# Graph attention on one core: addresses read a run ahead, one-hots of two batches, sums of sixteen tiles

## The chip, the cores and the metric

The kernel runs on one core of a Trainium2 chip. The metric is the device time of one execution in microseconds. The names of the engines are those of the profile: PE (TensorE, with PEld for its weight loads), DVE (VectorE), ACT (ScalarE), POOL (GpSimd, here the issuer of the gathers), SP (issuer of most DMAs).

## The reference

A graph has 6250 nodes with 128 features and 206250 directed edges, sorted by destination, of which each has 128 features too. Every edge takes a key and a value from its source node, a query from its destination node and a factor from its own features; there are eight heads of 16.

```python
score = jnp.einsum('ehd,ehd,ehd->eh', Kh[src], Qh[dst], Eh) * inv_sqrt_d
score = jnp.exp(jnp.clip(score, -5.0, 5.0))
msg = Vh[src] * score[:, :, None]
wV = jax.ops.segment_sum(msg, dst, num_segments=N)
Z = jax.ops.segment_sum(score, dst, num_segments=N)
h_out = wV / (Z[:, :, None] + 1e-06)
x = _layernorm(x + h_out)
```

## The kernel before

**Tiles and batches.** The edges are cut into 1612 tiles of 128 (one edge a partition), and these into 406 batches: 401 of four tiles, then small ones. The loop at L591 goes over the batches and works on several at once: for batch b it issues PE's products (`stage_a`, L463), for batch b-1 DVE's (`stage_b`, L478) and ACT's exps (`weigh`, L493), for batch b-2 the messages (`messages`, L523) and their sums (`stage_c`, L530).

**What a batch needs.** `gather` (L410) has POOL fetch the key and value rows of each tile's source nodes, one indirect DMA a tile, into one of 12 buffers `kvrows`. For batches from 12 on the rows come from the table kv, which the kernel builds at the start (`table`, L270: PE's `kvacc`, copies `kvst` by ACT and DVE, stores by SP); the first 12 batches gather rows of x and project them. A gather of batch b also waits for the PE product `qps` of batch b - lag(b), where lag (L360) falls from 12 to 3. For 163 tiles, the last ones of chosen batches, no gather is issued: ACT (88 columns, L392) and DVE (40 columns, L389, two at a time) copy columns of x from SBUF into a tile `xcol`, by addresses that each engine loads into its registers (L382, TENSOR_LOAD, eight addresses a run), and PE projects them (L401); ACT copies the result (L408).

**The chain of one batch.** PE makes `eps` = edge features times WE (L471, one PSUM buffer) and `qps` = queries spread over the edges (L474), whose left side is the one-hot `onehotT` (`stage_0t`, L454: DVE compares bf16 offsets `relb` with a node number). DVE then multiplies kq = kvrows × qps (L481) and kqe = kq × eps (L484), sums over a head (L487) and clips (L490). ACT takes the exp twice (L497, L498), DVE multiplies msg (L525), PE adds msg into `agg` (L547) with the one-hot `onehot` (`stage_0`, L444: DVE compares 64 node numbers with `rel`) on the left. Between these instructions `fill` (L583) puts single steps of other work on DVE: parts of the query table (`q_rows`, L301) and of finished blocks' layernorm (L741).

**Windows and sums.** Destinations are sorted, so a tile's nodes lie in a window of 64 from `window_start`. Four tiles share a window start; two groups of four (a pair, eight tiles) share one accumulator column, the second group 16 nodes on, with its 64 one-hot columns in the upper half of the 128; two such columns make an `agg` of 272 elements, which ACT copies to `sum` (L553). When all windows that touch two blocks of 128 nodes are there, `finish` (L513) has PE shift and add them into `finps` (L510), ACT copy that to `fin` (L520), and the layernorm steps are queued for the next round, the first of them rz (L749).

**What sets the order.** Up to batch 12 the framework orders the instructions; from then on (L592) each engine runs them in the order of the program. An instruction that waits holds up all behind it on its engine; SP's loads and stores are one such list, POOL's gathers another. Edge features (`ea`) are loaded in chunks of eight tiles into a ring of five buffers (L346).

**The window of destinations.** `from_window` (L183) prepares the bf16 offsets: it loads destinations (`dB_sb`), takes a bounded start (L191), subtracts (L194), stores the result to HBM (relD, read back as `relb`) and counts. Its first half runs while the tables are built, its second from batch 30 on, a step a batch.

Of the kernel before, what the change touches and what calls it, by code (L numbers as in the profile page):

```python
# [9 lines left out]
F32 = mybir.dt.float32  # L10
I32 = mybir.dt.int32
BF16 = mybir.dt.bfloat16
# [11 lines left out]
HW = 64  # L24
HALF = 16
DRIFT = 24
# [6 lines left out]
GLEAD = 2  # L33
OHB = (3, 5)
TAIL = 8
# [20 lines left out]
RING = 4096  # L56
SUMS = 8
XT_AT = RING + P
# [20 lines left out]

def pair_of(t):  # L80

    return (t // (2 * G), t // G % 2) if t < LAST else (NT, 1)


def pair_start(k):

    return (2 * k * G * N + NT // 2) // NT - DRIFT


def window_start(t):  # L90
    k, half = pair_of(t)
    return QL * P + HW if k == NT else pair_start(k) + HALF * half

# [7 lines left out]
def edge_attention(ctx: ExitStack, tc: tile.TileContext, x, xT, srcT, srcC, dstT, dstB, dst0, bnd, lo, eaT,  # L101
# [37 lines left out]
    with ExitStack() as fast:  # L139
# [7 lines left out]
        nc.gpsimd.iota(io2, pattern=[[1, P]], base=0, channel_multiplier=0)  # L147
        nc.vector.tensor_scalar(shift[:HW], io_i[:HW], 0, None, op0=ALU.is_equal)
        nc.vector.tensor_scalar(shift[HW:], io_i[HW:], HALF - HW, None, op0=ALU.is_equal)
        nc.vector.tensor_scalar(ident, io_i[:, P:2 * P], 0, None, op0=ALU.is_equal)  # L150
        for h in range(2):
            for tl in halves[h]:
                nc.vector.memset(tl[:, :, HW - HW * h:P - HW * h], 0.0)
        nc.vector.tensor_copy(iota_f, io2)
        dB_sb = [ip.tile([P, WT * P], I32, name="dB_sb", bufs=1)]
        nc.scalar.dma_start(dB_sb[0][:min(P, NJ)], dstB[:min(P, NJ)])
        bnd_c = ip.tile([P, (NJ + P - 1) // P], I32, name="bnd_c")
# [25 lines left out]
        def from_window(i):  # L183

            a, k = i * P, min(P, NJ - i * P)
            if i == len(dB_sb):
                dB_sb.append(ip.tile([P, WT * P], I32, name="dB_sb", bufs=1))
                nc.sync.dma_start(dB_sb[i][:k], dstB[a:a + k])
            d = dB_sb[i]
            w = ip.tile([P, 1], F32, name="wq0", bufs=2)  # L190
            nc.vector.tensor_tensor(w[:k], d[:k, :1], bnd_c[:k, i:i + 1], op=ALU.min)  # L191
# [172 lines left out]
        col_tiles, xT_bytes = {}, spread.bitcast(U8)  # L364
        used = [0, 0]

        copied, projected = {}, []

        def columns(eng, b, share=1.0):
# [5 lines left out]
            due = int((b - COL0 + COLL - 1 + share) * runs * COLP[1] / COLP[0] + 1e-6)  # L375
            while copied.get(engine, 0) < min(due, len(col_batches) * runs):
                k, j = divmod(copied.get(engine, 0), runs)
                copied[engine] = copied.get(engine, 0) + 1
                if k not in col_tiles:
                    col_tiles[k] = wp.tile([P, P], F32, name="xcol", bufs=4)  # L380
                to, j = col_tiles[k].bitcast(U8), first + j * size
                at = nc.values_load_multi_w_load_instructions(  # L382
                    col_at[k % col_half:k % col_half + 1, k // col_half, j:j + size], engines=(engine,),
                    min_val=XT_AT, max_val=XT_AT + 8 * (N - 1) + 4,
                    skip_runtime_bounds_check_because="edges name nodes")[1]
# [44 lines left out]
        def project(g, n):  # L430
# [6 lines left out]
            for i in range(0, n, 2):  # L437
# [4 lines left out]
                nc.scalar.copy(g[:, i:i + k, :], pk[:, :k, :])  # L442

        def stage_0(b):  # L444
            t0, n = batches[b][0], len(batches[b])
            half = pair_of(t0)[1]
            oh = halves[half][used[half] % OHB[half]]
            used[half] += 1
            nc.vector.tensor_tensor(oh[:, :n, HW * half:HW * half + HW],  # L449
                                    iota_p[:, None, :].to_broadcast([P, n, HW]),  # L450
                                    rel[:, t0:t0 + n, None].to_broadcast([P, n, HW]), op=ALU.is_equal)
            st8[b] = oh, None

        def stage_0t(b):  # L454
            t0, n = batches[b][0], len(batches[b])
            oh = st8[b][0]
            ohT = wp.tile([QROWS, B * P], BF16, name="onehotT", bufs=AHEAD + 2)
            e0 = t0 % RC * P
            nc.vector.tensor_scalar(ohT[:, :n * P], rels[t0 // RC][:, e0:e0 + n * P], node[:QROWS], None,  # L459
                                    op0=ALU.is_equal)  # L460
            st8[b] = oh, ohT

# [38 lines left out]
        def windows(q):  # L501

            return [(k, pair_start(k) - q * P) for k in range(min(NT, LAST + 2 * G - 1) // (2 * G))
                    if -HW - HALF < pair_start(k) - q * P < P]

        def add_windows(ps, q, first, stop):

            parts = windows(q)
            for i, (k, s) in enumerate(parts):
                nc.tensor.matmul(ps, shift[:, P - s:2 * P - s], sums[k // 2][:, k % 2],  # L510
                                 start=first and i == 0, stop=stop and i == len(parts) - 1)

        def finish(j):  # L513
# [5 lines left out]
            fin = sp.tile([P, 2, MW], F32, name="fin", bufs=2)  # L519
            nc.scalar.copy(fin, ps)  # L520
            pending.append(layernorm(nc, sp, fin, xbs.pop(q), out, q, 2, stores))

# [7 lines left out]
        def stage_c(b):  # L530
            n, g, oh, m = st8.pop(b)
            for i in range(n):
                t = batches[b][i]
                k, half = pair_of(t)
                q = t * N // NT // P
# [3 lines left out]
                final = k == NT  # L539
                u = k if final else k // 2  # L540
                first = u not in aggs
                if first:
                    aggs[u] = psA.tile([P, 2, MW], F32, name="agg")
                    if final:
                        add_windows(aggs[u][:, 0], QL, True, False)
                tail = k == NT if t == NT - 1 else pair_of(t + 1)[0] != k
                nc.tensor.matmul(aggs[u][:, 0 if final else k % 2], oh[:, i, :], m[:, i, :],  # L547
                                 start=not final and t % (2 * G) == 0, stop=tail)
                if tail and final:
                    norms.insert(0, layernorm(nc, sp, aggs.pop(u)[:, :1], xbs.pop(QL), out, QL, 1, stores))  # L550
                elif tail and (k % 2 == 1 or t == LAST - 1):
                    sums[u] = sp.tile([P, 2, MW], F32, name="sum", bufs=SUMS)
                    nc.scalar.copy(sums[u][:, :k % 2 + 1], aggs.pop(u)[:, :k % 2 + 1])  # L553
                    while len(finished) < QL // 2 and all(v // 2 <= u for v, _ in windows(2 * len(finished) + 1)):
                        ready.append(len(finished))
                        finished.append(u)

# [33 lines left out]
        for b in range(nbat + 3):  # L591
# [225 lines left out]
```

## Time and profile before

| what | us |
|---|---|
| median of 3 runs (1856.61 to 1858.39) | 1858.12 |
| the profiled execution | 1862.53 |
| its span | 1860.7 |
| busy in it: PE | 1330.8 |
| busy in it: DVE | 1680.8 |
| busy in it: ACT | 1632.9 |
| busy in it: POOL | 1385.7 |

The profile shows one execution. Its rows by group give line, engine, operation, output and inputs, count, then busy time and mean ns of one, then the engine's idle time before them and what ended it. Timeline rows give start, duration, engine, line, operation, and in brackets the idle time before with its releaser. Rows of stretches give the stretch, its length, an engine's busy time and instructions in it, the granted clock, the DMA share and GB/s. The moved bytes are 378.43 MB, 203 GB/s on average, and the granted clock is 0.922 on average.

### The profile page before, as it was taken

To read this page: it belongs to the slowest core of one execution; us is meant where nothing else is said; L and a number is where in the kernel's file an instruction comes from. 1 tells how busy PE (TensorE), PEld (TensorE's weight loads), DVE (VectorE), ACT (ScalarE), POOL (GpSimd) and SP (SyncE) were. 2 spreads that over 40 slices of the span, in tenths; PEclk is the share of its full clock that TensorE was granted. 3 is DMA by queue.
4 is the path that set the end of the run, shared out by engine and by line. 5 is a ranking of instruction groups with operands and counts; after the bars stand their busy time and mean duration, and the time that the engine had idled before them with its cause. 6 is when DMAs were issued, how large, how long until landed. Compare 5 with 4: busy or idle time off the path is not lost.

```text
span 1860.7 us, 48856 instructions
## 1 busy us (share of the span) xinstructions
PE 1330.8 (72%) x9376; PEld 1158.3 (62%) x9376; DVE 1680.8 (90%) x6913; ACT 1632.9 (88%) x15519; POOL 1385.7 (74%) x1456
## 2 busy tenths in 40 slices
PE   6887577677776777776776776766777767666776
PEld 4776466566665666665665665656666656656665
DVE  5589799999999999999999999989998999998987
ACT  2339689899999999999999999999999999998992
POOL 6777677777777777777777777777777777777774
PEclk7998799899999999999999899998898999998998
DMA  9776657667776576677677667667766676667662
GB/s 299 213 230 196 180 173 214 199 203 205 209 215 204 178 238 202 187 219 224 192 210 227 190 198 222 198 185 217 215 207 181 204 222 192 194 197 226 204 195 70
DMA packets 171231, 378.43 MB, mean 203 GB/s; under 512 B 58622, under 2 KB 84556, under 8 KB 170918
## 3 DMA queue, kind: packets, MB, share of 16 engines
q0 software_dynamic: 68768, 186.80, 34.6%
q1 hardware_dynamic: 101010, 187.38, 33.1%
q14 instruction: 237, 1.94, 0.3%
q8 instruction: 76, 1.25, 0.3%
q10 hardware_dynamic: 1140, 1.06, 0.2%
HBM read 360.30 MB, written 14.81 MB: 202 GB/s over the span
## 4 chain that ended last, share of the span: by engine, by line
DVE 43%; PE 11%; DMA 11%; issue 6%; DVEq 5%; POOL 4%; ACT 2%; ACTq 0%; POOLq 0%
DMA kvrows<-kv,src 11%; DVE kqe L484 8%; DVE kq L481 8%; DVE xcol L389 7%; DVE sc L487 5%; DVE msg L525 5%; DVEq L382 5%; PE eps L471 4%; DVE onehot L449 4%; POOL kvrows L419 4%; DVE onehotT L459 3%; PE finps L510 3%; PE agg L547 2%; DVE sc L490 1%; ACT xcol L392 1%
## 5 line engine op out<-in xcount | busy, mean ns | idle before, releaser
L419 POOL DMA_INDIRECT kvrows<-kv,src x1401 | 1338.9, 956 | 434.4 <-issue 305.5
L392 ACT COPY xcol<-xT_sb 128x4 uint8 x14344 | 1442.5, 191 | 44.7 <-issue 37.3
L471 PE MATMUL eps<-we_sb,ea 128*128 128x128 f32 x3224 | 489.5, 298 | 456.6 <-issue 224.0
L471 PEld LDWEIGHTS eps<-we_sb,ea 128*128 128x128 f32 x3224 | 425.8, 205 | 549.8 <-issue 458.4
L547 PE MATMUL agg<-msg,onehot 128*128 128x136 f32 x3224 | 533.9, 313 | 35.8 <-DVE msg L525 24.9
L547 PEld LDWEIGHTS agg<-msg,onehot 128*128 128x128 f32 x3224 | 454.5, 211 | 88.9 <-DVE msg L525 86.5
L389 DVE TENSOR_TENSOR xcol<-xT_sb 128x8 uint8 x3260 | 298.8, 159 | 25.1 <-issue 22.8
L481 DVE TENSOR_TENSOR kq<-kvrows,qps 128x512 f32<-128x512 f32 x406 | 274.4, 676 | 46.5 <-DMA kvrows<-kv,src 25.3
L484 DVE TENSOR_TENSOR kqe<-kq,eps 128x512 f32<-128x512 f32 x406 | 272.9, 672 | 2.5 <-PE eps L471 2.1
L525 DVE TENSOR_TENSOR msg<-kvrows,exp_p 128x512 f32<-128x512 f32 x406 | 272.2, 670 | 2.7 <-ACT exp_p L498 2.6
L487 DVE TENSOR_REDUCE sc<-kqe 128x32 f32<-128x512 f32 x406 | 271.1, 668 | 0.4
L449 DVE TENSOR_TENSOR onehot<-iota_p,dst_sb 128x256 f32<-128x256 f32 x406 | 167.3, 413 | 3.2 <-PE agg L547 3.2
L474 PE MATMUL qps<-qw,onehotT 126*128 126x128 bf16 x1612 | 168.8, 229 | 0.0
L459 DVE TENSOR_SCALAR onehotT<-relb,node 126x512 bf16<-126x512 bf16 x406 | 148.6, 367 | 4.6 <-PE qps L474 3.8
L497 ACT ACTIVATE msg<-sc 128x32 f32<-128x32 f32 x406 | 92.8, 229 | 66.0 <-DVE sc L490 61.7
L474 PEld LDWEIGHTS <-onehotT 126*128 126x128 bf16 x1612 | 134.8, 104 | 8.7
L401 PE MATMUL colkv<-wkv_sb,xcol 128*128 128x256 f32 x326 | 108.7, 418 | 0.0
L490 DVE TENSOR_SCALAR sc<-sc 128x32 f32<-128x32 f32 x406 | 82.2, 202 | 0.2
L510 PE MATMUL finps<-sum,shift 128*128 128x136 f32 x640 | 81.0, 285 | 0.0
L510 PEld LDWEIGHTS finps<-sum,shift 128*128 128x128 f32 x640 | 77.5, 194 | 0.0
L498 ACT ACTIVATE exp_p<-sc 128x32 f32<-128x32 f32 x406 | 74.0, 182 | 0.0
L419 POOL DMA_INDIRECT kvrows<-x,src x48 | 45.9, 955 | 20.6 <-issue 12.8
(76 smaller groups left out, 569.1 us busy)
## 6 DMA issues: line engine op xcount, KB each, us to landing
ea<-eaT SPq DMA_DIRECT2D x201, 512.0 KB
relb<-relD SPq DMA_DIRECT2D x100, 504.0 KB
kvrows<-kv,src POOLq DMA_INDIRECT x1401
qw<-qs SPq DMA_DIRECT2D x202, 31.5 KB
kv<-kvst SPq DMA_DIRECT2D x12, 512.0 KB
qs<-qst SPq DMA_DIRECT2D x48, 96.0 KB
xst<-xT SPq DMA_DIRECT2D x12, 256.0 KB
xb<-x SPq DMA_DIRECT2D x24, 128.0 KB
```

The lines of the kernel that those rows point to most:

```text
L389: eng.tensor_tensor(to[:, 4 * (j + c):4 * (j + c) + 8], *both, op=ALU.bitwise_or)
L392: copy(to[:, 4 * (j + c):4 * (j + c) + 4], xT_bytes[:, ds(at[c] - XT_AT, 4)])
L419: ins = nc.gpsimd.indirect_dma_start(out=g[:k, i, :f], out_offset=None, in_=rows, in_offset=bass.IndirectOffsetOnAxis(ap=src_col(t)[:k], a ...
L449: nc.vector.tensor_tensor(oh[:, :n, HW * half:HW * half + HW], iota_p[:, None, :].to_broadcast([P, n, HW]), rel[:, t0:t0 + n, None].to_bro ...
L471: nc.tensor.matmul(pe[:, i, :], ea[:, i * P:i * P + P], we_sb, start=True, stop=True)
L474: expanded[b] = nc.tensor.matmul(pq[:, i, :], ohT[:, i * P:i * P + P], loaded[t0 // WT], start=True, stop=True)
L481: nc.vector.tensor_tensor(t0[:, :n], g[:, :n, :D], pq[:, :n], op=ALU.mult)
L484: nc.vector.tensor_tensor(t1[:, :n], t0[:, :n], pe[:, :n], op=ALU.mult)
L487: nc.vector.tensor_reduce(sc[:, :n], t1[:, :n].rearrange("p b (h d) -> p b h d", h=H), axis=AX.X, op=ALU.add)
L510: nc.tensor.matmul(ps, shift[:, P - s:2 * P - s], sums[k // 2][:, k % 2], start=first and i == 0, stop=stop and i == len(parts) - 1)
L525: nc.vector.tensor_tensor(m[:, :n, :D].rearrange("p b (h d) -> p b h d", h=H), g[:, :n, D:].rearrange("p b (h d) -> p b h d", h=H), exp_p[ ...
L547: nc.tensor.matmul(aggs[u][:, 0 if final else k % 2], oh[:, i, :], m[:, i, :], start=not final and t % (2 * G) == 0, stop=tail)
```

## The change

- `columns`: each engine keeps a list of loaded runs of addresses and loads one run further than the one it copies.
- `finish` no longer issues the copy to `fin`; the copy, and the queueing of the layernorm, come behind the exps of the same round (`blocks_out`).
- `stage_0` and `stage_0t` make the one-hots of two batches in one instruction (`together`) in every other round; in the rounds between, DVE's column work of half a batch and of a whole batch stands in those two places.
- A window start still serves four tiles, but sixteen tiles share one accumulator of 136 elements, each four 16 nodes on from the four before (QUAD, STEPS). A one-hot tile has 64 zero columns ahead and 64 behind each tile's own 64, and the 128 columns that PE reads are shifted. `sum` holds 136 elements; there are nine buffers in place of eight.
- `from_window`: `dB_sb` takes a slot of the `ea` ring in place of a buffer of its own; the first load is issued when the function first runs, and in the second half three steps lie between the load and the first use.

```diff
-HALF = 16
+QUAD = 4
+STEPS = 16
-OHB = (3, 5)
+OHB = 5
-SUMS = 8
+XCOLS = 4
+SUMS = 9
...
-def pair_of(t):
-    return (t // (2 * G), t // G % 2) if t < LAST else (NT, 1)
-def pair_start(k):
-    return (2 * k * G * N + NT // 2) // NT - DRIFT
+def window_of(t):
+    return (t // (QUAD * G), STEPS * (t // G % QUAD)) if t < LAST else (NT, HW)
+def first_node(k):
+    return (QUAD * k * G * N + NT // 2) // NT - DRIFT
...
-    halves = [[cp.tile([P, B, P], F32, name=f"onehot{h}{i}") for i in range(OHB[h])] for h in range(2)]
+    onehots = [cp.tile([P, HW + 2 * B * P], F32, name=f"onehot{i}") for i in range(OHB)]
...
-        dB_sb = [ip.tile([P, WT * P], I32, name="dB_sb", bufs=1)]
-        nc.scalar.dma_start(dB_sb[0][:min(P, NJ)], dstB[:min(P, NJ)])
         bnd_c = ip.tile([P, (NJ + P - 1) // P], I32, name="bnd_c")
         nc.scalar.dma_start(bnd_c, bnd[1:].rearrange("o (g p) -> p (o g)", p=P))
...
         def from_window(i):
             a, k = i * P, min(P, NJ - i * P)
-            if i == len(dB_sb):
-                dB_sb.append(ip.tile([P, WT * P], I32, name="dB_sb", bufs=1))
-                nc.sync.dma_start(dB_sb[i][:k], dstB[a:a + k])
-            d = dB_sb[i]
+            d = ep.tile([P, WT * P], I32, name="dB_sb", tag="ea")
+            (nc.sync if i else nc.scalar).dma_start(d[:k], dstB[a:a + k])
+            if i:
+                yield
+                yield
+                yield
             w = ip.tile([P, 1], F32, name="wq0", bufs=2)
...
-            tl = ep.tile([P, CH * P], F32, name="ea")
+            tl = ep.tile([P, CH * P], F32, name="ea", tag="ea")
...
-                at = nc.values_load_multi_w_load_instructions(
-                    col_at[k % col_half:k % col_half + 1, k // col_half, j:j + size], engines=(engine,),
...
+                known = addresses.setdefault(engine, [])
+                while len(known) < 2 and fetched.get(engine, 0) < total:
+                    kf, jf = divmod(fetched.get(engine, 0), runs)
+                    fetched[engine] = fetched.get(engine, 0) + 1
+                    jf = first + jf * size
+                    known.append(nc.values_load_multi_w_load_instructions(
+                        col_at[kf % col_half:kf % col_half + 1, kf // col_half, jf:jf + size], engines=(engine,),
...
+                at = known.pop(0)
...
+        def together(b):
+            t0 = batches[b][0]
+            n = len(batches[b])
+            if n == B and b + 1 < nbat and len(batches[b + 1]) == B and t0 % (2 * B) == 0:
+                return [b, b + 1]
+            return [] if n == B and t0 % (2 * B) else [b]
...
         def stage_0(b):
-            t0, n = batches[b][0], len(batches[b])
+            group = together(b)
+            if not group:
+                return
+            t0, n = batches[b][0], sum(len(batches[i]) for i in group)
...
-            ohT = wp.tile([QROWS, B * P], BF16, name="onehotT", bufs=AHEAD + 2)
+            ohT = wp.tile([QROWS, 2 * B * P], BF16, name="onehotT", bufs=3)
...
         def finish(j):
...
             fin = sp.tile([P, 2, MW], F32, name="fin", bufs=2)
-            nc.scalar.copy(fin, ps)
-            pending.append(layernorm(nc, sp, fin, xbs.pop(q), out, q, 2, stores))
+
+            def copied_out():
+                nc.scalar.copy(fin, ps)
+                pending.append(layernorm(nc, sp, fin, xbs.pop(q), out, q, 2, stores))
+
+            blocks_out.append(copied_out)
...
-                    aggs[u] = psA.tile([P, 2, MW], F32, name="agg")
+                    aggs[k] = psA.tile([P, 1, MW], F32, name="agg")
...
-                nc.tensor.matmul(aggs[u][:, 0 if final else k % 2], oh[:, i, :], m[:, i, :],
-                                 start=not final and t % (2 * G) == 0, stop=tail)
+                nc.tensor.matmul(aggs[k][:, 0], oh[0][:, oh[1] + i * P:oh[1] + i * P + P], m[:, i, :],
+                                 start=not final and t % (QUAD * G) == 0, stop=tail)
...
-            if b + AHEAD < nbat:
+            if b + AHEAD < nbat and together(b + AHEAD):
                 stage_0(b + AHEAD)
+            elif b < nbat:
+                columns(nc.vector, b, 0.5)
             fill()
             next(steps, None)
-            if b + AHEAD < nbat:
+            if b + AHEAD < nbat and together(b + AHEAD):
                 stage_0t(b + AHEAD)
+            elif b < nbat:
+                columns(nc.vector, b, 1.0)
...
             if 0 <= b - 1 < nbat:
                 weigh(b - 1)
+            while blocks_out:
+                blocks_out.pop(0)()
             if b < nbat:
                 columns(nc.scalar, b)
```

More of the change, by code (lines that the diff above doesn't have):

```diff
@@ L147, in edge_attention @@
         nc.gpsimd.iota(io2, pattern=[[1, P]], base=0, channel_multiplier=0)
[L148 to L149 removed]
+        nc.vector.tensor_scalar(shift, io_i, 0, None, op0=ALU.is_equal)
         nc.vector.tensor_scalar(ident, io_i[:, P:2 * P], 0, None, op0=ALU.is_equal)
[L151 to L153 removed]
+        for tl in onehots:
+            nc.vector.memset(tl[:, :HW], 0.0)
+            nc.vector.memset(tl[:, HW:].rearrange("p (t n) -> p t n", n=P)[:, :, HW:], 0.0)
         nc.vector.tensor_copy(iota_f, io2)
[L155 to L156 removed]
         bnd_c = ip.tile([P, (NJ + P - 1) // P], I32, name="bnd_c")
@@ L364, in edge_attention @@
         col_tiles, xT_bytes = {}, spread.bitcast(U8)
-        used = [0, 0]
+        used = [0]
         copied, projected = {}, []
+        addresses, fetched = {}, {}
         def columns(eng, b, share=1.0):
@@ L375, in columns @@
             due = int((b - COL0 + COLL - 1 + share) * runs * COLP[1] / COLP[0] + 1e-6)
-            while copied.get(engine, 0) < min(due, len(col_batches) * runs):
+            total = len(col_batches) * runs
+            while copied.get(engine, 0) < min(due, total):
                 k, j = divmod(copied.get(engine, 0), runs)
@@ L460, in stage_0t @@
                                     op0=ALU.is_equal)
-            st8[b] = oh, ohT
+            for i in group:
+                tl, at, _ = st8[i]
+                k = (batches[i][0] - t0) * P
+                st8[i] = (tl, at), ohT[:, k:k + len(batches[i]) * P]
         def stage_a(b, g):
@@ L501, in windows @@
         def windows(q):
-            return [(k, pair_start(k) - q * P) for k in range(min(NT, LAST + 2 * G - 1) // (2 * G))
-                    if -HW - HALF < pair_start(k) - q * P < P]
+            return [(k, first_node(k) - q * P) for k in range((LAST - 1) // (QUAD * G) + 1)
+                    if -HW - STEPS * (QUAD - 1) < first_node(k) - q * P < P]
         def add_windows(ps, q, first, stop):
@@ L509, in add_windows @@
             for i, (k, s) in enumerate(parts):
-                nc.tensor.matmul(ps, shift[:, P - s:2 * P - s], sums[k // 2][:, k % 2],
+                nc.tensor.matmul(ps, shift[:, P - s:2 * P - s], sums[k],
                                  start=first and i == 0, stop=stop and i == len(parts) - 1)
+        blocks_out = []
         def finish(j):
@@ L533, in stage_c @@
                 t = batches[b][i]
-                k, half = pair_of(t)
+                k, _ = window_of(t)
                 q = t * N // NT // P
@@ L539, in stage_c @@
                 final = k == NT
-                u = k if final else k // 2
-                first = u not in aggs
-                if first:
-                    aggs[u] = psA.tile([P, 2, MW], F32, name="agg")
+                if k not in aggs:
+                    aggs[k] = psA.tile([P, 1, MW], F32, name="agg")
                     if final:
-                        add_windows(aggs[u][:, 0], QL, True, False)
-                tail = k == NT if t == NT - 1 else pair_of(t + 1)[0] != k
-                nc.tensor.matmul(aggs[u][:, 0 if final else k % 2], oh[:, i, :], m[:, i, :],
-                                 start=not final and t % (2 * G) == 0, stop=tail)
+                        add_windows(aggs[k][:, 0], QL, True, False)
+                tail = t == NT - 1 or window_of(t + 1)[0] != k
+                nc.tensor.matmul(aggs[k][:, 0], oh[0][:, oh[1] + i * P:oh[1] + i * P + P], m[:, i, :],
+                                 start=not final and t % (QUAD * G) == 0, stop=tail)
                 if tail and final:
[L550 to L554, printed above, removed]
+                    norms.insert(0, layernorm(nc, sp, aggs.pop(k), xbs.pop(QL), out, QL, 1, stores))
+                elif tail:
+                    sums[k] = sp.tile([P, MW], F32, name="sum", bufs=SUMS)
+                    nc.scalar.copy(sums[k], aggs.pop(k)[:, 0])
+                    while len(finished) < QL // 2 and all(v <= k for v, _ in windows(2 * len(finished) + 1)):
                         ready.append(len(finished))
-                        finished.append(u)
+                        finished.append(k)
         for b0 in range(0, 4 * KB, KB):
```

26 lines of the change are left out of this document (14 added, 12 removed).

## The prediction

> **What bounds the kernel now.** I read the page first: busy shares, the chain, the costliest groups.
>
> ```profile
> PE 1330.8 (72%) x9376; PEld 1158.3 (62%) x9376; DVE 1680.8 (90%) x6913; ACT 1632.9 (88%) x15519; POOL 1385.7 (74%) x1456
> DVE 43%; PE 11%; DMA 11%; issue 6%; DVEq 5%; POOL 4%; ACT 2%; ACTq 0%; POOLq 0%
> L419 POOL DMA_INDIRECT kvrows<-kv,src x1401 | 1338.9, 956 | 434.4 <-issue 305.5
> L419 POOL DMA_INDIRECT kvrows<-x,src x48 | 45.9, 955 | 20.6 <-issue 12.8
> ```
>
> By shares DVE (90%) and ACT (88%) look like the bound, and the change works on them. But POOL's idle time is odd: 434.4 + 20.6 = 455.0 us before 1449 gathers, 0.31 us each, mostly "issue", so waiting for nothing. The timeline of POOL shows whether that gap ever closes, and the stretches (busy time, number of gathers, clock, DMA share, GB/s) whether the rate ever changes.
>
> ```profile
> 1603.12 0.95 POOL L419 DMA_INDIRECT kvrows<-kv,src  x1 [0.30 <-issue]
> 1604.38 0.94 POOL L419 DMA_INDIRECT kvrows<-kv,src  x1 [0.30 <-DMA kvrows<-kv,src]
> ...
> 199.00:254.00 55.00, 37.67 (x38) 0.78 0.64 188
> 254.00:400.00 146.00, 110.17 (x115) 0.93 0.66 193
> 400.00:1800.00 1400.00, 1060.68 (x1113) 0.93 0.69 206
> ...
> 3.61 1.11 POOL L419 DMA_INDIRECT kvrows<-x,src  x1 [2.04 <-DMA src<-srcT]
> ...
> 1840.40 0.91 POOL L419 DMA_INDIRECT kvrows<-kv,src  x1 [0.30 <-issue]
> ```
>
> Starts are 1.26 us apart, 0.95 busy plus 0.30. From 400 to 1800 us, 1113 gathers take 1400 us: 1.258 us each, never resting. So POOL at "74%" is full. Its work is fixed: 1449 × 1.258 = 1822.8 us. It runs from 3.6 to 1841.3, which is 1837.7 us. **All that POOL loses in the whole run is 14.9 us**; 19.4 us of tail follow (span 1860.7).
>
> Do DVE and ACT follow POOL? The product L481 runs once a batch, so its counts give the batch rate.
>
> ```profile
> 400.00:1200.00 800.00, 125.59 (x185) 0.94 0.70 208
> 1200.00:1800.00 600.00, 91.14 (x134) 0.93 0.69 202
> ```
>
> A batch needs 1449/406 = 3.57 gathers, 4.49 us of POOL. From 400 to 1200 DVE and ACT take 800/185 = 4.32 us a batch and eat up the gathers' lead; from 1200 on they take 600/134 = 4.48 us, POOL's rate. There they wait for rows already, and faster DVE or ACT work buys only a longer wait. The gain must come from POOL's 14.9 us and from the tail.
>
> **Where POOL loses time, and what the change does there.**
>
> ```profile
> 36.84 0.94 POOL L419 DMA_INDIRECT kvrows<-x,src  x1 [4.33 <-PE kvacc L278]
> ...
> 214.41 1.44 POOL L419 DMA_INDIRECT kvrows<-kv,src  x1 [4.34 <-PE eps L471]
> ...
> 249.09 1.06 POOL L419 DMA_INDIRECT kvrows<-kv,src  x1 [1.22 <-PE qps L474]
> ...
> 253.86 0.95 POOL L419 DMA_INDIRECT kvrows<-kv,src  x1 [1.21 <-PE qps L474]
> ...
> 349.74 0.95 POOL L419 DMA_INDIRECT kvrows<-kv,src  x1 [1.11 <-PE eps L471]
> ```
>
> Less the usual 0.30, the last four hold 4.04 + 0.92 + 0.91 + 0.81 = 6.7 us; the first, 4.0 us, belongs to the start. The rest are stretched gathers, further down. The 4.34 has its cause on DVE:
>
> ```profile
> 195.49 0.26 SPq L188 DMA_DIRECT2D dB_sb<-dstB  x1
> ...
> 210.43 0.15 DVE L191 TENSOR_TENSOR wq<-dB_sb,bnd_c 74x1 f32<-74x1 int32 x1 [11.23 <-DMA dB_sb<-dstB]
> ```
>
> DVE stood 11.23 us at L191 for the second load of dB_sb. All products queued behind it, PE's eps and qps behind these, and POOL, which had run through its lead, stopped until 214.41. **The three yields** put L191 three batches behind its load: 3 × 4.32 = 13.0 us, more than the 11.2 waited. With DVE 11 us further on, the small waits until 350 us go as well. Term: −6.7 us, bounds −6.7 and 0. If the load lands late, POOL's lead, which outlasted 11 us of standstill here before it ran out, covers it. What is late next is POOL itself. The load takes a slot of the ea ring; the slot's chunk was read by PE some batches before, so SP's queue, where ea, relb, qw and the stores stand behind it, should not wait.
>
> **The first dB_sb load** loses its early place on ACT's queue and has no yields ahead of its L191.
>
> ```profile
> 3.36 0.33 ACTq L156 DMA_DIRECT2D dB_sb<-dstB  x1
> ...
> 13.93 0.15 DVE L191 TENSOR_TENSOR wq<-dB_sb,bnd_c 128x1 f32<-128x1 int32 x1
> ```
>
> Today L191 waits for nothing, at 13.93. A later load stops DVE there, with the kvst copies (L281) behind it, then kvacc on PE, to which POOL's early gathers are paced (the 4.33 above). Bounds: +7 (the 11.2 wait of the second load, the nearest row, less the 4.0 that POOL loses anyway) and −4 (these 4.0 go, since bnd_c, starts and bnd_r come earlier and one ea chunk starts later in the crowded beginning). The order is written by hand only from the twelfth batch on, and the load depends on nothing, so it can still run early: I take 0.
>
> **One-hots of two batches.** Durations overlap on DVE, so I use starts:
>
> ```profile
> 1010.68 0.42 DVE L449 TENSOR_TENSOR onehot<-iota_p,dst_sb 128x256 f32<-128x256 f32 x1
> 1011.02 0.68 DVE L484 TENSOR_TENSOR kqe<-kq,eps 128x512 f32<-128x512 f32 x1
> 1011.61 0.35 DVE L459 TENSOR_SCALAR onehotT<-relb,node 126x512 bf16<-126x512 bf16 x1
> 1011.88 0.68 DVE L487 TENSOR_REDUCE sc<-kqe 128x32 f32<-128x512 f32 x1
> ...
> L459 DVE TENSOR_SCALAR onehotT<-relb,node 126x512 bf16<-126x512 bf16 x401 | 146.9, 367 | 4.6 <-PE qps L474 3.8 <-DMA relb<-relD 0.7
> L459 DVE TENSOR_SCALAR onehotT<-relb,node 126x128 bf16<-126x128 bf16 x2 | 0.5, 246 | 0.0
> ```
>
> A 128x256 one-hot takes 0.34 to the next start, kqe with 512 elements 0.59: two become one, −0.09 us a pair. onehotT costs 0.27; its two widths give (367 − 246)/384 = 0.32 ns an element, so 1024 elements cost 0.27 + 0.16 = 0.43 against 0.54: −0.11, and 0 if it scaled fully. Some 203 pairs × 0.20 = 41 us of DVE, or 18. On the time: 0, because DVE then waits for gathers. Without that cover it would be the whole 41.
>
> **Finished blocks, sums.**
>
> ```profile
> L510 PE MATMUL finps<-sum,shift 128*128 128x136 f32 x640 | 81.0, 285 | 0.0
> L520 ACT COPY fin<-finps 128x272 f32<-128x272 f32 x24 | 9.3, 386 | 31.6 <-PE finps L510 31.5
> L749 DVE TENSOR_SCALAR rz<-fin 128x16 f32<-128x16 f32 x24 | 4.7, 195 | 39.3 <-ACT fin L520 39.3
> ...
> 1838.44 3.91 PE L510 MATMUL finps<-sum,shift 128*128 128x136 f32 x24
> ...
> 1842.80 0.17 DVE L749 TENSOR_SCALAR rz<-fin 128x16 f32<-128x16 f32 x1 [3.57 <-ACT fin L520]
> ```
>
> By the windows' formulas finps falls from 640 instructions to 370, from 24 to 28 a pair of blocks to 14 or 16. The copy fin then stands behind two exps (ACT no longer waits 1.3 us for PE ahead of them), with the column copies behind it and DVE's rz waiting for it: at worst the two exps later, against some 1.3 us saved on PE. Within the loop that trims ACT's 31.5 and DVE's 39.3 us, on the time 0, by the same cover. In the tail nothing covers: the last block stops DVE for 3.57 us, until 1842.80, when POOL is already done. There 24 instructions become 16: 3.91 × 8/24 = 1.3 us less, and some of the rest goes because DVE's next products no longer wait for exps behind the copy. Term: −2 us, bounds −3.6 (the whole wait) and 0.
>
> **Column addresses and the rest.**
>
> ```profile
> L382 ACTq TENSOR_LOAD <-col_at x1793: 537/553/1048, 131.0 to 1821.8; - x200
> L382 DVEq TENSOR_LOAD <-col_at x815: 591/606/1081, 132.4 to 1820.9; - x163
>   issue: 22.8, 74
> ```
>
> Their number stays; only their place moves. What the engines show of waits before column work is small (DVE's 22.8 us in 74 waits). With columns ahead of kqe in every other batch, PE's eps comes up to 0.4 us later there; DVE and ACT still have 0.17 us a batch in hand against POOL, and more by what was saved above. Term 0. Gathers stay 1449, and DMA bytes stay.
>
> **A lock against the change.** Some gathers are stretched while DVE works:
>
> ```profile
> 784.30 0.34 DVE L459 TENSOR_SCALAR onehotT<-relb,node 126x512 bf16<-126x512 bf16 x1
> 784.34 1.13 POOL L419 DMA_INDIRECT kvrows<-kv,src  x1 [0.30 <-DMA kvrows<-kv,src]
> ...
> L419 POOL DMA_INDIRECT kvrows<-kv,src x1401: 907/949/2050, 68.6 to 1840.4; - x176
> ```
>
> A gather that began 0.04 us behind onehotT took 1.13 instead of 0.95: held until 0.22 us after onehotT's start. Doubled, with 0.16 us more, it would hold until 0.38. At random phase that is today 406 × 0.22/1.258 = 71 hits × 0.11 = 7.8 us, and then 203 × 0.38/1.258 = 61 × 0.19 = 11.7 us: +3.9. But the mean (956) is only 7 ns above the median (949), 10 us in all from every cause, so fewer are hit than at random; I take +1.5, bounds −2 (half as many ops) and the rival below. The Trainium skill ("SBUF — State Buffer", section "SBUF: two separate sides") says that VectorE in a two-port mode and GpSimd share a port pair as an exclusive lock, held for the whole instruction. This row agrees in kind, though 0.22 us is less than the 0.34 of the whole op; by whole instructions the doubled op would hold some 0.5 us, random phase would add about 4 us more, and the sum below would be some −1 to −3, by my estimate.
>
> **Sum.** −6.7 + 0 − 2 + 1.5 = −7.2 us. The profiled execution, 1862.53 us (span 1860.7 and 1.8 around it), becomes 1855.3. It lies 4.4 us above the median of the runs, so on their scale: 1858.1 − 7.2 = **1851 us**.
>
> **Rivals.**
> - *DVE and ACT are the bound after all.* Then the savings land: 41 (one-hots) + 11 (dB_sb) + 23 (issue) + about 30 of the 39.3 = 105 us, 1753 us. For it: 90% and DVE's 43% of the chain. Against: POOL's constant 1.258 us, and 4.48 us a batch from 1200 on. 4%.
> - *The start gives it back.* The first dB_sb load stops DVE and POOL by the upper bound: −7.2 + 7 = 0, 1858 us; or the waits of 214 to 350 us come back, because POOL meets its lead's limit anyway. For it: DMA is crowded there and no yield covers it. Against: the load is free to go early. 18%.
> - *Slower: the doubled onehotT locks POOL.* DVE now keeps step with the gathers, so its phase against them may stay put and hit over and over. Without the lock term the sum is −8.7; at 0.19 us a hit it takes 46 hits beyond today's to eat that. Half of the 203: 19.4 us, 1858.1 − 8.7 + 19.4 = 1869 us; all: 38.6 us, 1888. For it: the row above. Against: DVE kept step from 1200 us on already, and the rate held. 12%.
>
> **How the numbers follow.** My forecast has 66%, with a range of its own of 1840 to 1856. Its low end is POOL's floor: all of the 14.9 us and the whole tail wait, −14.9 − 3.6 = −18.5, which is below the terms' own bounds (−6.7 − 4 − 3.6 − 2 = −16.3); its high end leaves −2 of the sum. A run of this kernel tells about 0.2%, 3.7 us, from no change, so "faster" begins below 1854.4. Faster: 4% and some 60 of the 66%. Same: the 18% and the rest of the 66%. Slower: 12%. The range of 8 in 10 reaches from 1840 to 1861 (the start's rival with 3 us of scatter), leaving out the first rival and the lock's.
>
> **What would show it.** Right: no DVE wait at L191 near 200 us, POOL without gaps from 69 us on, 1113 gathers or one or two more from 400 to 1800, DVE busy down by some 40 us while its waits for kvrows grow by more than that, rz's waits down. Wrong: a steady POOL interval other than 1.258 (up: the lock; down: POOL was not at its limit), POOL waits for qps or eps that remain after 69 us, or L191 waiting near 14 us with kvacc late.

## The result, and the profile after

The changed kernel took a median of 1853.56 us (17 runs, 1851.63 to 1857.43), the kernel before beside it 1859.02 us (17 runs, 1856.61 to 1862.93): a ratio of 0.9971 [0.9964, 0.9979], 5.5 us less. Of the three chips that the later runs met, two took 1.39 times as long for the kernel before (2582.8 to 2590.0 us), so each kernel below is compared with the one before on its own chip, and the two are called the slower chips.

The profiled execution of after took 1852.51 us, 1.0 below its median; that of before lay 3.5 above its own. So the two profiles differ by 10.0 us, and 4.5 of these belong to the pick of the executions. The page after, busy shares, chain and the gathers:

```profile
PE 1306.9 (71%) x9104; PEld 1134.8 (61%) x9104; DVE 1655.5 (89%) x6514; ACT 1626.7 (88%) x15519; POOL 1385.6 (75%) x1456
...
DVE 38%; DMA 15%; PE 14%; ACT 12%; issue 8%; POOL 6%; DVEq 4%; ACTq 2%; SPq 0%; POOLq 0%
...
L429 POOL DMA_INDIRECT kvrows<-kv,src x1401 | 1338.0, 955 | 427.4 <-issue 318.7
...
L429 POOL DMA_INDIRECT kvrows<-x,src x48 | 46.6, 971 | 20.5 <-issue 11.6
```

DVE works 25.3 us less. POOL's busy time on the gathers is as before (1384.6 against 1384.8), its idle time ahead of them 447.9 against 455.0: 7.1 us less. The stretches of POOL, columns as before (length, busy, gathers, clock, DMA share, GB/s):

```profile
199.00:254.00 55.00, 41.59 (x45) 0.91 0.74 222
254.00:400.00 146.00, 110.97 (x116) 0.91 0.69 201
400.00:1800.00 1400.00, 1060.69 (x1113) 0.92 0.70 205
```

The gain stands in the first row: 45 gathers between 199 and 254 us, where 38 were. From 400 to 1800 us there are 1113, as before, to the gather. And POOL hardly ever waits. The row of its gaps at "issue" (us in all, times, longest), and the only gap behind 37.63 us that is longer than 0.33 us:

```profile
POOL kvrows L429 <- issue: 330.3, 1084, 0.3
...
1036.24 0.94 POOL L429 DMA_INDIRECT kvrows<-kv,src  x1 [0.83 <-DMA kvrows<-kv,src]
```

The batches, by the product L507 in the same stretches as before:

```profile
400.00:1200.00 800.00, 125.58 (x184) 0.94 0.70 206
1200.00:1800.00 600.00, 90.83 (x133) 0.91 0.70 203
```

They were 185 and 134. With 25 us less to do, DVE does not go through the batches any faster. The timeline of the changed kernel at four places:

```profile
17.81 0.23 DVE L192 TENSOR_TENSOR wq<-dB_sb,bnd_c 128x1 f32<-128x1 int32 x1 [5.29 <-DMA dB_sb<-dstB]
...
37.63 0.94 POOL L429 DMA_INDIRECT kvrows<-x,src  x1 [4.30 <-PE kvacc L279]
...
211.84 0.15 DVE L192 TENSOR_TENSOR wq<-dB_sb,bnd_c 74x1 f32<-74x1 int32 x1 [2.72 <-DMA dB_sb<-dstB]
...
1830.61 2.07 PE L536 MATMUL finps<-sum,shift 128*128 128x136 f32 x16
...
1833.13 0.17 DVE L785 TENSOR_SCALAR rz<-fin 128x16 f32<-128x16 f32 x1
1833.18 0.90 POOL L429 DMA_INDIRECT kvrows<-kv,src  x1 [0.31 <-PE agg L577]
```

The first load of dB_sb now does hold DVE, for 5.29 us, but POOL's wait of the start is what it was (4.30 against 4.33), though it ends 0.8 us later. The second still holds DVE for 2.72 us in place of 11.23, and POOL doesn't notice. The last gather ends at 1834.08 instead of 1841.31 (-7.2), and the tail behind it is 16.6 us instead of 19.4 (-2.8): that is the whole difference of the spans, 10.0.

### The profile page after: what moved, and what is told of

Same layout as the page of the kernel before. It is cut to its first block, busy times and chain, and to the rows that moved or that the text cites. A ratio compares the mean times of both kernels' runs of the same rounds, so it can differ in the third digit from the quotient of the medians.

```text
span 1850.7 us, 47948 instructions
## 1 busy us (share of the span) xinstructions
PE 1306.9 (71%) x9104; PEld 1134.8 (61%) x9104; DVE 1655.5 (89%) x6514; ACT 1626.7 (88%) x15519; POOL 1385.6 (75%) x1456
## 4 chain that ended last, share of the span: by engine, by line
DVE 38%; DMA 15%; PE 14%; ACT 12%; issue 8%; POOL 6%; DVEq 4%; ACTq 2%; SPq 0%; POOLq 0%
DMA kvrows<-kv,src 13%; ACT xcol L402 10%; DVE xcol L399 7%; DVE kqe L510 7%; DVE kq L507 6%; POOL kvrows L429 6%; DVE sc L513 6%; PE eps L497 5%; DVEq L391 4%; PE agg L577 4%; DVE msg L557 3%; DVE onehot L469 3%; DVE onehotT L482 2%; ACTq L391 2%; PE kvps L451 1%
## 5 line engine op out<-in xcount | busy, mean ns | idle before, releaser
L429 POOL DMA_INDIRECT kvrows<-kv,src x1401 | 1338.0, 955 | 427.4 <-issue 318.7
L402 ACT COPY xcol<-xT_sb 128x4 uint8 x14344 | 1447.0, 191 | 52.1 <-issue 45.3
L497 PE MATMUL eps<-we_sb,ea 128*128 128x128 f32 x3224 | 499.6, 303 | 416.4 <-DVE kqe L510 243.7
L497 PEld LDWEIGHTS eps<-we_sb,ea 128*128 128x128 f32 x3224 | 435.3, 209 | 510.5 <-issue 351.4
L507 DVE TENSOR_TENSOR kq<-kvrows,qps 128x512 f32<-128x512 f32 x406 | 275.7, 679 | 82.6 <-DMA kvrows<-kv,src 33.8
L399 DVE TENSOR_TENSOR xcol<-xT_sb 128x8 uint8 x3260 | 312.9, 162 | 26.8 <-issue 21.1
L469 DVE TENSOR_TENSOR onehot<-iota_p,dst_sb 128x512 f32<-128x512 f32 (+2 forms) x206 | 138.2, 672 | 2.0 <-PE agg L577 2.0
L482 DVE TENSOR_SCALAR onehotT<-relb,node 126x1024 bf16<-126x1024 bf16 (+2 forms) x206 | 102.7, 499 | 3.3 <-DMA relb<-relD 1.8
L429 POOL DMA_INDIRECT kvrows<-x,src x48 | 46.6, 971 | 20.5 <-issue 11.6
L418 ACT COPY kvrows<-colkv 128x256 f32<-128x256 f32 x163 | 58.9, 361 | 1.4 <-PE colkv L411 1.3
L411 PEld LDWEIGHTS colkv<-wkv_sb,xcol 128*128 128x128 f32 x326 | 56.9, 215 | 0.0
## 6 DMA issues: line engine op xcount, KB each, us to landing
qw<-qs SPq DMA_DIRECT2D x202, 31.5 KB
```

Of the source, the lines that this page charges most:

```text
L411: nc.tensor.matmul(pk, col_tiles.pop(k), wkv_sb, start=True, stop=True)
L429: ins = nc.gpsimd.indirect_dma_start(out=g[:k, i, :f], out_offset=None, in_=rows, in_offset=bass.IndirectOffsetOnAxis(ap=src_col(t)[:k], a ...
L469: nc.vector.tensor_tensor(tl[:, HW:].rearrange("p (t n) -> p t n", n=P)[:, :n, :HW], iota_p[:, None, :].to_broadcast([P, n, HW]), rel[:, t ...
L497: nc.tensor.matmul(pe[:, i, :], ea[:, i * P:i * P + P], we_sb, start=True, stop=True)
L507: nc.vector.tensor_tensor(t0[:, :n], g[:, :n, :D], pq[:, :n], op=ALU.mult)
```

## The experiments

**Theory A** is that of the prediction: POOL's issue of gathers is the bound, so the three yields bring the gain, the work saved on DVE and ACT brings nothing, and tail and lock about cancel. **Rival B**: DVE and ACT set the pace, the saved work brings the gain, and the yields hardly any. The yields also spare DVE most of its 11.23 us wait, so a gain from them would not speak against DVE by itself. What tells the two apart is whether the 25 us that the rest saves on DVE bring anything on top.

**The yields alone**, on the kernel before, no other part of the change:

```diff
                 nc.sync.dma_start(dB_sb[i][:k], dstB[a:a + k])
+                yield
+                yield
+                yield
```

First on a slower chip, twice:

> The kernel before with the three steps between the second dB_sb load and its first use, nothing else of the change. Theory A (POOL's issue of the gathers sets the end, only what frees POOL counts): the waits of POOL between 199 and 254 us go, -6 us against before (range -4 to -9), without any of the saved DVE or ACT work. Theory B (the gain is what is left of the work saved on DVE and ACT): at most -2 us.

Measured: 0.9985 [0.9958, 1.0013] (2585.1 against 2589.95 us).

> The kernel before with the three steps behind the second dB_sb load, once more, on a chip where the kernel before takes about 1859 us again. Theory A (POOL's issue of the gathers sets the end): -6 us against before (range -4 to -9). Theory B (the gain is what is left of the work saved on DVE and ACT): at most -2 us.

Measured: 0.9974 [0.9950, 0.9999] (2580.13 against 2584.9 us). Neither decides anything about the chip that the prediction was made for. The third did:

> The kernel before with the three steps behind the second dB_sb load. If the kernel before takes about 1859 us here: theory A (POOL's issue of the gathers sets the end) -6 us (range -4 to -9), theory B (the gain is what is left of the work saved on DVE and ACT) at most -2 us. If it takes about 2585 us again, with POOL busy for little more than half of the time, theory A has POOL waiting for the other engines there, and both give at most -11 us, 0.4%.

Measured, where before took 1859.15 us: 1853.11 us (1851.76 to 1855.16), 0.9969 [0.9958, 0.9981]. The whole change had 0.9971 [0.9964, 0.9979]. **Three lines do all that the change does to the time**; what the rest adds is nothing within some 2.5 us, where 25 us less of a DVE that set the pace would be ten times that. The profile of yields alone, the stretches of POOL first, then its groups and two places of its timeline:

```profile
199.00:254.00 55.00, 42.02 (x43) 0.87 0.74 218
254.00:400.00 146.00, 110.67 (x117) 0.89 0.67 201
400.00:1800.00 1400.00, 1060.47 (x1115) 0.93 0.68 205
```

```profile
L422 POOL DMA_INDIRECT kvrows<-kv,src x1401 | 1336.3, 954 | 426.9 <-issue 306.9 <-DVE msg L528 13.7 <-PE qps L477 13.7
...
L422 POOL DMA_INDIRECT kvrows<-x,src x48 | 45.8, 954 | 21.3 <-issue 11.9 <-PE kvacc L281 6.5 <-DMA src<-srcT 2.0
```

```profile
212.66 0.15 DVE L194 TENSOR_TENSOR wq<-dB_sb,bnd_c 74x1 f32<-74x1 int32 x1 [3.00 <-DMA dB_sb<-dstB]
...
1831.00 0.90 POOL L422 DMA_INDIRECT kvrows<-kv,src  x1 [0.30 <-issue]
...
1832.83 0.17 DVE L752 TENSOR_SCALAR rz<-fin 128x16 f32<-128x16 f32 x1 [2.09 <-ACT fin L523]
```

43 gathers between 199 and 254 us, and 1115 from 400 to 1800 with the old one-hots. DVE is busy for 1680.5 us in it, as in before; the 25 us that the whole change saves there are worth nothing. Behind 42.73 us no gather waits longer than 0.36 us, so POOL's own interval and its stretched gathers set its end. So ACT, whose work the change leaves nearly as it is, isn't the bound either. POOL ends at 1831.90, 2.2 us ahead of the whole change, and the tail takes 19.3 us, 2.7 more than the whole change. Those two cancel.

**The rest without the yields.** The complement was meant to show the same from the other side:

```diff
-            if i:
-                yield
-                yield
-                yield
```

> The changed kernel without the three steps: L192 waits for its load at once again, all other parts stay. Theory A: POOL stands still near 210 us again, and the gain shrinks to the tail's -3 us plus the lock's +3: 0 us against before (range -3 to +3). Theory B: the gain stays, -4 to -6 us against before.

> The changed kernel without the three steps, once more. Theory A: 0 us against before (range -3 to +3), POOL standing still near 210 us. Theory B: -4 to -6 us against before.

> The changed kernel without the three steps: all of the saved DVE, ACT and PE work stays, and L192 waits for its load at once again. Theory A (POOL's issue of the gathers sets the end): POOL stands still near 210 us again, 0 us against before (range -3 to +3). Theory B (the gain is what is left of the saved work): -4 to -6 us.

All three fell on the slower chips and gave 0.9815 [0.9759, 0.9870] (2538.63 us), 0.9830 [0.9793, 0.9867] (2543.39) and 0.9824 [0.9783, 0.9866] (2542.97). There the rest of the change gains 1.8%, 40 to 51 us by the medians, and the yields nearly nothing: theory A would be wrong there. The page of the first of them shows that it isn't the same case:

```profile
PE 1592.3 (63%) x9104; PEld 1398.4 (55%) x9104; DVE 1695.1 (67%) x6514; ACT 1712.4 (67%) x15519; POOL 1379.9 (54%) x1456
...
ACT 45%; issue 22%; PE 9%; DVE 8%; ACTq 6%; another core or an unknown queue 4%; DMA 2%; DVEq 1%; POOL 1%; SPq 0%; POOLq 0%
```

Its waits, the longest one:

```profile
ACT xcol L398 <- issue: 564.9, 1013, 1.2
```

and the same wait in the changed kernel:

```profile
ACT xcol L402 <- issue: 45.3, 155, 1.2
```

The busy times of DVE, ACT and POOL are within some 5% of the changed kernel's, PE's is 22% longer. But ahead of its column copies ACT stands for 565 us in 1013 waits, and POOL, at 54%, now waits for others. It comes with the chip and not with the edit, for the yields alone have run on both kinds, first where before takes 1859 us, then on a slower chip:

```profile
ACT xcol L395 <- issue: 36.4, 132, 0.8
...
ACT xcol L395 <- issue: 566.7, 1011, 1.2
```

Two kernels tested on a slower chip whether ACT is the bound there. One issues DVE's clip of sc three times instead of once, the other ACT's exp_p twice, both on the changed kernel, with its yields:

```diff
+            nc.vector.tensor_scalar(sc[:, :n], sc[:, :n], -20.0, 20.0, op0=ALU.max, op1=ALU.min)
+            nc.vector.tensor_scalar(sc[:, :n], sc[:, :n], -20.0, 20.0, op0=ALU.max, op1=ALU.min)
```

```diff
+            nc.scalar.activation(exp_p[:, :n], sc[:, :n], AF.Exp, scale=0.25)
```

> The changed kernel with the clip of sc issued three times in place of once (the same result): about 0.17 us more DVE work a batch, 69 us in all, more than the change saved on DVE. Theory A: DVE still keeps below POOL's 4.49 us a batch, so 0 to +5 us against the changed kernel (-5 to 0 against before). Theory B: +50 to +69 us.

> The changed kernel with the second exp (into exp_p) issued twice (the same result): some 0.13 us more ACT work a batch, 53 us in all. ACT's 4.34 us a batch in the stretch 400 to 1200 becomes 4.47, just below POOL's 4.49. Theory A: 0 to +8 us against the changed kernel. Theory B with ACT as the bound: +50 us.

> The changed kernel with the clip of sc issued three times in place of once (the same result): about 0.17 us more DVE work a batch, 69 us in all. Theory A: DVE keeps below POOL's 4.49 us a batch, so 0 to +5 us against the changed kernel (-6 to 0 against before). Theory B: +50 to +69 us.

The changed kernel as it stands never ran on a slower chip; the nearest without an addition are the kernels without yields, and the yields alone moved the medians there by 0.2%. DVE's addition: 0.9832 [0.9781, 0.9883] and 0.9812 [0.9770, 0.9855], against 0.9815 and 0.9824. ACT's: 1.0227 [1.0176, 1.0278], 110 us more (2648.77 against 2538.63). The pages of the two, DVE's addition first:

```profile
PE 1588.9 (63%) x9104; PEld 1394.9 (55%) x9104; DVE 1856.7 (74%) x7326; ACT 1712.4 (68%) x15519; POOL 1385.5 (55%) x1456
```

```profile
PE 1661.1 (63%) x9104; PEld 1450.7 (55%) x9104; DVE 1701.5 (64%) x6514; ACT 1799.5 (68%) x15925; POOL 1380.9 (52%) x1456
```

On the slower chips 162 us more of DVE cost nothing and 87 us more of ACT cost 110. So the time there hangs on ACT and not on POOL, and runs there say nothing on theory A. Why ACT's instructions reach it so late there was not found (its address loads have a median of 0.553 us there and 0.554 on the other chip), nor which part of the change gains the 40 to 51 us.

**More columns, fewer gathers.** If POOL is the bound, work taken from POOL should pay, until DVE runs out of time. Here 13 gathers more are replaced by columns, and DVE takes 48 columns of each such tile instead of 40, ACT 80 instead of 88:

```diff
-COLP = (7, 3)
-COLA = (8, 11)
-COLV = (8, 5)
+COLP = (13, 6)
+COLA = (8, 10)
+COLV = (8, 6)
```

> The changed kernel with 176 column tiles in place of 163 (6 in 13 batches), 80 columns of each on ACT and 48 on DVE: 13 gathers fewer for POOL, about as much work for ACT, 8% more of the column work... on DVE 0.23 us a batch more. Theory A: 13 x 1.258 = -16 us against the changed kernel, -22 against before (range -14 to -24). Theory B: slower than the changed kernel, +40 us or more by DVE's added work.

On a slower chip: 0.9650 [0.9614, 0.9687] (2492.46 against 2582.76 us). ACT has 264 copies fewer, which fits. The like on the kernel before (COLP (25, 12), same split):

> The kernel before with 183 column tiles (12 in 25 batches), 80 columns on ACT and 48 on DVE: 20 gathers fewer, 25 us less of POOL's work. Without the change's savings DVE needs some 4.5 us a batch by its rows (4.13 busy + 0.3 for the columns + its loads and waits), more than POOL's 4.43. Theory A: DVE and ACT become the bound, so only a part of the 25 us comes: -15 to +10 us against before. Theory B: +60 us or more.

On the same chip: 0.9987 [0.9962, 1.0012] (2581.44 us). That fits less well: ACT has 296 copies of 0.19 us more, some 56 us, and the time stays, while its issue waits are 514 us, fewer than the 567 of yields alone. So ACT's copies alone don't set the time on these chips. And where before takes 1858:

> The changed kernel with 176 column tiles in place of 163 (6 in 13 batches), 80 columns of each on ACT and 48 on DVE: 13 gathers fewer for POOL, about the same column work for ACT, 0.23 us a batch more for DVE (some 90 us in all, twice what the change saved there). If the kernel before takes about 1859 us here: theory A (POOL's issue of the gathers sets the end, the work saved on DVE was only cover) 13 x 1.258 = -16 us against the changed kernel, -22 against before (range -14 to -24), POOL still at 1.258 us a gather. Theory B (DVE and ACT set the pace): slower than the changed kernel, by 40 us or more.

**That expectation was wrong**, and its theory B named the time. 1947.46 us (1944.73 to 1953.71) against 1858.18, 1.0477 [1.0457, 1.0497]: 94 us more than the changed kernel. The stretches, POOL's L429, then DVE's L507, the groups, the queue's loads and three waits of this kernel:

```profile
400.00:1800.00 1400.00, 991.38 (x1041) 0.89 0.65 192
```

```profile
400.00:1200.00 800.00, 115.96 (x170) 0.89 0.65 191
1200.00:1800.00 600.00, 88.74 (x130) 0.89 0.65 192
```

```profile
L429 POOL DMA_INDIRECT kvrows<-kv,src x1388 | 1324.8, 954 | 539.6 <-issue 330.9 <-PE qps L500 80.4 <-DVE sc L516 23.9
...
L399 DVE TENSOR_TENSOR xcol<-xT_sb 128x8 uint8 x4224 | 407.4, 163 | 87.9 <-issue 79.2
```

```profile
L391 DVEq TENSOR_LOAD <-col_at x1056: 591/606/998, 128.7 to 1915.7; - x176
```

```profile
DVE xcol L399 <- issue: 79.2, 216, 1.0
...
DVE kq L507 <- DMA kvrows<-kv,src: 3.4, 4, 1.8
...
POOL kvrows L429 <- PE qps L500: 80.4, 77, 5.1
```

Now POOL waits for PE's qps in 77 places, its interval goes to 1400/1041 = 1.345 us, and the batches take 800/170 = 4.71 us. DVE's kq waits 3.4 us in all for gathered rows, in place of 33.8: DVE is the bound in this kernel. It doesn't bring theory B back for the changed kernel, where POOL has one gap longer than 0.33 us behind 45 us; here it has 127, which exceed 0.30 by 117 us in all. Against the changed kernel's row of the same group,

```profile
L399 DVE TENSOR_TENSOR xcol<-xT_sb 128x8 uint8 x3260 | 312.9, 162 | 26.8 <-issue 21.1
```

DVE has 94.5 us more of column work and 58.1 more of issue waits ahead of it: 152.6/406 = 0.38 us a batch, on top of 800/184 = 4.35. That is 4.73, and 4.71 was measured; but 4.35 need not be DVE's own pace, since 25 us less of its work didn't shorten it, so the agreement is no proof of the split. My expectation set 0.23 us a batch of DVE's busy time against a margin of 0.14, and left out the waits that came with 241 more address loads of 0.606 us on DVE's queue. So the margin that covered everything else in this study is thin: 4.49 us of POOL a batch against 4.35 of DVE and ACT.

## Why the prediction was right, point by point

The direction, the cause and the size were right: 5.5 us of gain for 7.2 predicted, 1853.6 for 1851. Two terms were too small and of opposite sign, the tail and the lock; that their errors cancel is luck. The single terms below are read from one execution of each kernel, and executions of one kernel spread by some 6 us. By the steps:

- **POOL is the bound, the work saved on DVE and ACT is worth 0.** Shown, by the 25.3 us of DVE adding nothing to the yields, by 1113 gathers from 400 to 1800 us in both kernels, and by POOL's gaps, which behind 38 us are longer than 0.33 us only once. That fewer gathers would save time was not shown: the one test of it here made DVE the bound.
- **The three yields, -6.7.** Alone, they measured -6.0 by medians; the waits of 214 to 350 us are gone in both kernels with yields. One thing in the working was off: the predicted wait of nothing at the second load is 2.72 us. The yields gave DVE 14.4 us (issue at 194.70, DVE there at 209.1), but the load took 17.1 us where it had taken 14.9. The cover named for that case, POOL's lead, held.
- **The first load, 0.** Nearly right on POOL. The fear was half true: DVE stands there for 5.29 us, and the wait for kvacc is within 0.03 us of before, but POOL's 61st and 121st gathers start 0.50 and 0.65 us later than before.
- **The tail, -2.** Measured -2.8: the 24 instructions of 3.91 us became 16 of 2.07, and rz waits for nothing instead of 3.57 us. DVE starts rz at 1833.13, ahead of the last gather's end at 1834.08; before, it came 1.5 us behind it.
- **The lock, +1.5.** Mis-sized. The two rows that show it:

```profile
783.72 0.48 DVE L482 TENSOR_SCALAR onehotT<-relb,node 126x1024 bf16<-126x1024 bf16 x1
783.82 1.20 POOL L429 DMA_INDIRECT kvrows<-kv,src  x1 [0.30 <-DVE kqe L510]
```

  A gather that began 0.10 us behind the doubled onehotT took 1.20 us instead of 0.95: it was held until 0.35 us after onehotT's start (0.10 and the 0.25 us by which the gather is longer than 0.95; 0.38 predicted). Taking from the timeline all gathers that began within 0.5 us behind an onehotT and took 1.00 us or more, their excess over 0.95 is 2.3 us in before, 2.2 with yields alone and 5.0 after: **+2.7 us**. In all 32 of them after, the hold ends 0.33 to 0.37 us behind onehotT's start; in 19 of the 22 of before, and in all 22 with yields alone, 0.21 to 0.24. Of 1.13 us and more there is one in before and 14 after. Half as many instructions, and twice the loss. All stretched gathers of the run, whatever the cause, exceed 0.95 us by 14.1 us after and 11.6 with yields alone; the difference is about the 2.2 us by which POOL ends later than with the yields alone. The prediction's side estimate for a hold of the whole instruction is too low: by its own formula, 0.50 us in place of 0.38 adds 203 × (0.50² − 0.38²)/(2 × 1.258) = 8.5 us at random phase, not 4. The hold of 0.35 us makes it moot. That undoing the doubling alone would give these back was not tried.
- **Finished blocks.** The groups of the changed kernel for fin, rz and finps:

```profile
L550 ACT COPY fin<-finps 128x272 f32<-128x272 f32 x24 | 9.2, 384 | 7.8 <-PE finps L536 7.7
...
L785 DVE TENSOR_SCALAR rz<-fin 128x16 f32<-128x16 f32 x24 | 4.3, 178 | 14.0 <-ACT fin L550 14.0
...
L536 PE MATMUL finps<-sum,shift 128*128 128x136 f32 x370 | 49.3, 287 | 0.0
```

  As predicted: 370 instructions, ACT's wait from 31.5 to 7.7 us, rz's from 39.3 to 14.0, and nothing on the time outside the tail. How much of it the copy's new place did was not separated.
- **Column addresses, 0.** Right on the time, and a gain of reading ahead can't be seen: the waits of issue ahead of DVE's columns went from 22.8 to 21.1 us, those of ACT from 37.3 to 45.3.
- **What failed is a sign that I had named:** DVE busy down by some 40 us, while its waits for kvrows grow by more than that. The rows of before, then of after:

```profile
L389 DVE TENSOR_TENSOR xcol<-xT_sb 128x8 uint8 x3260 | 298.8, 159 | 25.1 <-issue 22.8
L481 DVE TENSOR_TENSOR kq<-kvrows,qps 128x512 f32<-128x512 f32 x406 | 274.4, 676 | 46.5 <-DMA kvrows<-kv,src 25.3 <-issue 6.8 <-ACT kvrows L442 6.7
...
L449 DVE TENSOR_TENSOR onehot<-iota_p,dst_sb 128x256 f32<-128x256 f32 x406 | 167.3, 413 | 3.2 <-PE agg L547 3.2
L459 DVE TENSOR_SCALAR onehotT<-relb,node 126x512 bf16<-126x512 bf16 x406 | 148.6, 367 | 4.6 <-PE qps L474 3.8 <-DMA relb<-relD 0.7
```

```profile
L507 DVE TENSOR_TENSOR kq<-kvrows,qps 128x512 f32<-128x512 f32 x406 | 275.7, 679 | 82.6 <-DMA kvrows<-kv,src 33.8 <-PE qps L500 26.7 <-issue 9.9
...
L469 DVE TENSOR_TENSOR onehot<-iota_p,dst_sb 128x512 f32<-128x512 f32 (+2 forms) x206 | 138.2, 672 | 2.0 <-PE agg L577 2.0
L482 DVE TENSOR_SCALAR onehotT<-relb,node 126x1024 bf16<-126x1024 bf16 (+2 forms) x206 | 102.7, 499 | 3.3 <-DMA relb<-relD 1.8 <-PE qps L500 1.3
```

  The two one-hots fell by 75.0 us of durations. With 399 instructions fewer (6913 to 6514), the overlaps of about 0.08 us that each had with the next went too (0.42 against 0.34 to the next start), 32 us: 43 net, which is the 41 predicted. But the column work, now in two shares between the products, is busy for 14.1 us more (298.8 to 312.9) and the four products and sums of the chain for 4.3. That leaves 24, and 25.3 was measured. The freed time then did not go to one wait: of kq's idle time, 36.1 us more, only 8.5 is for gathered rows; 20 or more is for PE's qps (15 waits of 5.1 us in all before, 43 of 26.7 after). That the idle time shows up wherever a chain held at POOL's pace happens to end last is my reading, not shown.

**Left open:** the doubled onehotT undone, the place of the fin copy, and reading ahead, each by itself; the whole change less the yields, and more work on ACT or DVE alone, where before takes 1859 us. No version that beats both kernels was found: the yields alone equal the whole change.

## What to carry to other kernels

An engine with a constant gap ahead of every instruction can be full at 75% busy, as POOL was here: count its instructions in a long stretch, and if the gap never grows and the count doesn't move when others get faster, take it for the bound. Then only two things pay, its own stalls and what lies behind its last instruction; here three yields ahead of one late load were worth a rewrite of four other parts. Before moving work onto an engine with time in hand, take its pace (time a round when it isn't held) and not its busy time, and add what its queue spends on the new work: with a margin of only 0.14 us in 4.49, an expected gain became 94 us of loss.

## What the runs showed of the hardware

- The hold that onehotT puts on a gather grows with its size: it ends 0.22 us behind onehotT's start at 126x512 and 0.35 at 126x1024, both times some 0.13 us ahead of the end of the instruction (0.34 and 0.48 us).
- On two of three chips the kernel before took 1.39 times as long. Of the yields alone there are traces from both kinds: on the slower, ACT stood at "issue" for 567 us in place of 36, and the granted clock was 0.76 in place of 0.92, but ACT was busy only 5% longer, DVE 3%, PE 23%. POOL's usual interval between gathers, 1.25 us, was the same on both. The same column edit on the same kernel was a gain there (0.9650) and a loss on the third chip (1.0477), where another engine is the bound.
- Address loads of 0.606 us on DVE's queue, though issued one run ahead, may not be hidden: 241 more of them, with the columns that they serve, went with 58 us more of waits before the columns.
